# A Mamba stage's start: the first image's statistics loaded ahead of the weights, the second image's placed later

## The chip, the cores and the metric

The kernel runs on one core of a Trainium2 chip. A core has five engines that each work through their own queue of instructions in order: TensorE (PE, with its weight loads PEld), VectorE (DVE), ScalarE (ACT), GpSimd (POOL) and SyncE (SP), which here issues all transfers between DRAM and the core's memory. The engines wait for one another by semaphores. The metric is the device time of one execution in microseconds. Before the change it is 4613.92 us, the median of six runs (4610.43 to 4615.99).

## The reference

The input x holds two images of 256 channels and 64 x 64 positions, so 4096 positions ("tokens") each. Two layers follow one another; cut to what matters:

```python
x = x + mamba(group_norm(x))       # layer 0
x = x + attention(group_norm(x))   # layer 1

def mamba(v):                                  # tokens (B, L, C)
    yn = layer_norm(v) * gamma + beta
    xm, z = split(yn @ W_in.T)                 # 512 channels each
    u = silu(conv1d_4_taps(xm) + conv_b)
    proj = u @ W_xp.T                          # dt (16), B (16), C (16)
    dt = softplus(proj[..., :16] @ W_dt.T + b_dt)
    h = exp(dt * A) * h + dt * u * B           # scan over the 4096 tokens, 16 states a channel
    ym = (sum_n(h * C) + u * D) * silu(z)
    y2 = ym @ W_out.T + yn
    return gelu(y2 @ W1.T + b1) @ W2.T + b2 + y2
```

group_norm takes mean and variance over groups of 8 channels and all 4096 positions of an image. So nothing of an image can be normalised before all of that image has been read once. The second image's statistics are needed only when the second image is reached.

## The kernel before

`mamba_stage` handles layer 0 for both images, `attention_block` layer 1 for each image in turn. In `mamba_stage` an image is cut into 8 tiles of 512 tokens; the 16 tiles follow one another, and the scan's state is carried from tile to tile.

The stage begins with a part written straight down: SP issues the loads of all weights and small vectors (L337 to L354, then the permutation matrix, W_dt and the pick matrix at L362, L376 and L382), and VectorE, ScalarE and GpSimd prepare constants from them: neg_a, the negative exponential of A_log (L358, L359); diag_d (L364); 16 tap matrices, each the identity times one tap of the convolution (L369); w_dt, split into a rounded half and a rest (L379, L380); pick (L383). Three of these sources sit for a while in the three buffers of the ring r_yn, which later hold the tiles' normalised inputs yn.

All further work is handed to a planner (class Plan). Each task is added with an engine, a due time in scan steps, a cost, what it reads and what it writes. The planner lists the tasks in the order in which a model with these costs would start them: of the tasks of one engine that are ready, the one with the earliest due time goes first, a task with another ScalarE function table counting as later by SWITCH, and none more than HORIZON ahead of the oldest task not yet started. Buffers come from rings of a fixed number. That list fixes the order on every engine; on the chip each engine waits only by semaphores. The costs and due times decide only the order.

`first(b, t, due)` loads tile t of image b into a buffer of r_h (five buffers, later used by the scan's states) and takes two `bn_stats` on VectorE, one for each 128 channels (L321). `group_norm(b, k, due)` aggregates an image's statistics (L412), averages over groups by a matmul with gmat, takes the root on ScalarE (L424, L425), and writes scales. Both images were due at the same early times:

```python
    for b in range(IMAGES):
        for t in range(NT):
            first(b, t, -60 + 10 * b)
```

`front(i)` prepares tile i: load of x into yn (L459), group normalisation (L457), mean over channels by a matmul with lnmat, centring (L471), squares (L474), the second matmul, 1/root (L479, L480), scale and shift (L488, L492), four projections with w_in and convolutions with the taps (`conv`), the projection w_xp, its two copies (L516, L517) and VectorE's rest half (L508), then `softplus` for each of four channel groups (L553 to L575), whose results dt and dtu are stored to DRAM and reloaded with each row repeated (L674). `gate` computes silu(z) (L587). `step(g)` is one of 32 scan steps of a tile: two decays on ScalarE (L710), products with B on GpSimd or VectorE (L716), two scans on VectorE (L721), the product with C on GpSimd (L727), and the sum over states on PE (L751, L753). `back(i)` does the output projection with w_out (L599), the two-layer network with w_1 (L621) and w_2 (L635), the statistics for layer 1, and the store. front(i + 1) is added before tile i's steps, so that it runs beside them.

The attention part takes its exponentials on ScalarE, its matmuls on PE, and sums on VectorE and GpSimd; the change doesn't touch it.

Of the kernel before, what the change touches and what calls it, by code (L numbers as in the profile page):

```python
# [11 lines left out]
F32 = mybir.dt.float32  # L12
# [7 lines left out]
P = 128  # L20
# [3 lines left out]
D = 32  # L24
# [77 lines left out]
class Plan:  # L102
# [26 lines left out]
    def add(self, engine, due, cost, emit, reads=(), writes=(), tables=(), lands=0.0):  # L129


        task = Plan.Task()
        task.engine, task.due, task.cost, task.emit = engine, due, cost, emit
        task.tables, task.lands, task.at = tables, lands, len(self.tasks)
        deps = set()
        reads, writes = list(self.keys(reads)), list(self.keys(writes))
        for key in reads:
            deps.add(self.writer.get(key))
        for key in writes:
            deps.add(self.writer.get(key))  # L140
            deps.update(self.readers.get(key, ()))
        for key in reads:
            self.readers.setdefault(key, []).append(task)
        for key in writes:
            self.writer[key], self.readers[key] = task, []
        deps -= {None, task}
        task.deps, task.behind = len(deps), []
        task.ready, task.start = 0.0, None
        for dep in deps:
            dep.behind.append(task)  # L150
        task.bufs = list({id(b): b for b, _ in reads + writes}.values())
        for buf in task.bufs:
            if buf.ring and not buf.left:
                buf.turn = buf.ring.asked
                buf.ring.asked += 1
            buf.left += 1
        self.tasks.append(task)
# [89 lines left out]
def mamba_stage(ctx, tc, xs, stats_out, consts, w, outs):  # L247
# [12 lines left out]
    nc = tc.nc  # L260
    ident, gmat, lnmat, eps_t = consts
    IMAGES = len(xs)
    C, L = xs[0].shape
    KC = C // P
    NT = L // T
    DI = w["conv_w"].shape[0]
    KD = DI // P
    R = w["W_dtT"].shape[0]
    NP = w["W_xpT"].shape[1]
    N = (NP - R) // 2  # L270
    HID = w["W1T"].shape[1]
    KH = HID // P
# [6 lines left out]
    NS = LOW + NP  # L279

    wp = ctx.enter_context(tc.tile_pool(name="l0w", bufs=1))
# [4 lines left out]
    def ring(name, bufs, n=1, pool=None, rows=P, dtype=F32, free=False):  # L286
        return Ring(pool or sb, [rows, T] if n == 1 else [rows, n, T], name, bufs, dtype, free)

    mm = ring("mm", 3, pool=ps, free=True)
    r_yn, r_u, r_z = ring("yn", 3, KC), ring("u", KD + 1), ring("z", KD)  # L290
# [7 lines left out]
    r_h, r_y = ring("h", 5, 2), ring("y", 1, pool=ps)  # L298
# [5 lines left out]
    add = plan.add  # L304

    def image_tile(x, t):
        return x.rearrange("(k p) l -> p k l", p=P)[:, :, bass.ts(t, T)]


    stats_in = [wp.tile([P, KC, NT, nc.vector.BN_STATS_DIM], F32, name=f"stats_in{b}") for b in range(IMAGES)]  # L310
    stats_bufs = [Buf(parts=KC * NT, tile=s) for s in stats_in]

    def first(b, t, due):
        xt = Buf(r_h)
        add("SP", due, 0.8, lambda: nc.sync.dma_start(xt.tile, image_tile(xs[b], t)), [], [xt], lands=3.0)
        for k in range(KC):
            add(
                "DVE",
                due,
                0.7,  # L320
                lambda k=k: nc.vector.bn_stats(stats_in[b][:, k, t, :], xt.tile[:, k, :]),  # L321
                [xt],
                [stats_bufs[b][k * NT + t]],
            )


    def load_rows(name, src, k):
        t = wp.tile([P, k, src.shape[1]], F32, name=name)
        nc.sync.dma_start(t, src.rearrange("(k p) f -> p k f", p=P))
        return t  # L330

    def load_vec(name, src, k):
        t = wp.tile([P, k], F32, name=name)
        nc.sync.dma_start(t, src.rearrange("(k p) -> p k", p=P))
        return t

    gamma = load_vec("gamma", w["gamma"], KC)  # L337
    beta = load_vec("beta", w["beta"], KC)
    w_in = load_rows("w_in", w["W_inT"], KC)
    conv_w = wp.tile([P, KD, TAPS], F32, name="conv_w")  # L340
    nc.sync.dma_start(conv_w, w["conv_w"].rearrange("(k p) o t -> p k (o t)", p=P))
    conv_b = load_vec("conv_b", w["conv_b"], KD)
    w_xp = load_rows("w_xp", w["W_xpT"], KD)
    b_dt = load_vec("b_dt", w["b_dt"], KD)
    d_vec = load_vec("d_vec", w["D"], KD)
    neg_a = wp.tile([P, KD, QUAD, NQ], F32, name="neg_a")
    nc.sync.dma_start(neg_a, w["A_log"].rearrange("p (k j q) -> p k j q", k=KD, j=QUAD))
    sum4 = wp.tile([P, PQ], F32, name="sum4")
    nc.sync.dma_start(sum4, w["sum4"])
    w_out = load_rows("w_out", w["W_outT"], KD)  # L350
    w_1 = load_rows("w_1", w["W1T"], KC)
    b_1 = load_vec("b_1", w["b1"], KH)
    w_2 = load_rows("w_2", w["W2T"], KH)
    b_2 = load_vec("b_2", w["b2"], KC)  # L354


# [1 line left out]
    nc.scalar.activation(neg_a, neg_a, AF.Exp)  # L358
    nc.vector.tensor_scalar_mul(neg_a, neg_a, -1.0)  # L359
    diag_d = wp.tile([P, KD, P], F32, name="diag_d")  # L360
    perm = r_yn.make()[:, 0, 0:P]
    nc.sync.dma_start(perm, w["perm"])  # L362
    for k in range(KD):
        nc.vector.tensor_scalar_mul(diag_d[:, k, :], perm, d_vec[:, k : k + 1])  # L364

# [6 lines left out]
    w_dt = wp.tile([NS, 2, DI], F32R, name="w_dt")  # L372
    nc.gpsimd.memset(w_dt.bitcast(F32), 0.0)
    pick = wp.tile([NS, NQ, P], F32R, name="pick")
    w_dt32 = r_yn.make()[:R, 0, :]
    nc.sync.dma_start(w_dt32, w["W_dtT"])  # L376
    for row in (0, LOW):
        rows = slice(row, row + R)
        nc.vector.tensor_copy(w_dt[rows, 0, :], w_dt32)  # L379
        nc.vector.tensor_sub(w_dt[rows, 1, :], w_dt32, w_dt[rows, 0, :].bitcast(F32))  # L380
    pick32 = r_yn.make()[:NS, 0, :]
    nc.sync.dma_start(pick32, w["pick"])  # L382
    nc.vector.tensor_copy(pick.rearrange("r q p -> r (q p)"), pick32)  # L383

    projs = [wp.tile([NS, T], F32R, name=f"proj{i}") for i in range(2)]
    for t in projs:
        nc.gpsimd.memset(t.bitcast(F32), 0.0)
    r_proj.make = itertools.cycle(projs).__next__

# [9 lines left out]
    def matmul(out, pairs):  # L401
        for i, (lhsT, rhs) in enumerate(pairs):
            nc.tensor.matmul(out, lhsT=lhsT, rhs=rhs, start=(i == 0), stop=(i == len(pairs) - 1))  # L403

    def group_norm(b, k, due):

        s = Buf(r_gn)
        p1, p2 = Buf(mm), Buf(mm)
        out = scales_buf[b * KC + k]

        def aggregate():
            nc.vector.bn_aggr(s.tile[:, 0:2], stats_in[b][:, k, :, :].rearrange("p a s -> p (a s)"))  # L412

        def spread():


            nc.vector.tensor_copy(s.tile[:, 2:3], p1.tile[:, 0:1])
            nc.vector.tensor_sub(s.tile[:, 3:4], s.tile[:, 0:1], s.tile[:, 2:3])
            nc.vector.scalar_tensor_tensor(
                s.tile[:, 4:5], s.tile[:, 3:4], s.tile[:, 3:4], s.tile[:, 1:2], ALU.mult, ALU.add  # L420
            )

        def root():
            nc.scalar.activation(s.tile[:, 5:6], p2.tile[:, 0:1], AF.Ln, bias=eps_t)  # L424
            nc.scalar.activation(scales[:, b, k, 1:2], s.tile[:, 5:6], AF.Exp, scale=-0.5)  # L425

        def shift():
            nc.vector.scalar_tensor_tensor(
                scales[:, b, k, 0:1], s.tile[:, 2:3], -1.0, scales[:, b, k, 1:2], ALU.mult, ALU.mult
            )  # L430

        add("DVE", due, 0.4, aggregate, [stats_bufs[b][k * NT + t] for t in range(NT)], [s])
        add("PE", due, 0.4, lambda: matmul(p1.tile[:, 0:1], [(gmat, s.tile[:, 0:1])]), [s], [p1])
        add("DVE", due, 0.6, spread, [p1], [s])
        add("PE", due, 0.4, lambda: matmul(p2.tile[:, 0:1], [(gmat, s.tile[:, 4:5])]), [s], [p2])
        add("ACT", due, 0.6, root, [p2], [s, out], ("exp",))
        add("DVE", due, 0.2, shift, [s], [out])
# [325 lines left out]
            add("DVE", g + 2.5, 0.7, lambda: nc.vector.tensor_mul(d.z[k].tile, y.tile, d.z[k].tile), [y], [d.z[k]])  # L763

    for b in range(IMAGES):
        for t in range(NT):
            first(b, t, -60 + 10 * b)
    for b in range(IMAGES):
        for k in range(KC):
            group_norm(b, k, -48 + 10 * b)  # L770
    front(0)
    for i, d in enumerate(tiles):
        d.z, d.b, d.c, d.dt_rep, d.dtu_rep = [], [], [], {}, {}
# [482 lines left out]
```

## Time and profile before

| | before |
|---|---|
| median of six runs | 4613.92 us |
| the profiled execution's own time | 4613.43 us |
| its span, first to last instruction | 4611.6 us |
| busy: PE | 4304.5 us (93%) |
| busy: VectorE | 3725.0 us (81%) |
| busy: ScalarE | 3658.3 us (79%) |
| busy: GpSimd | 3882.8 us (84%) |
| moved by DMA | 379.67 MB, 82 GB/s over the span |

The profile is one execution taken by the hardware profiler. Busy time of an engine is an average over two stages with different limits: the Mamba stage (the first 2,000 us or so) and attention. Instruction times are in microseconds from the start of the span; a line number is that of the kernel before. In a list of instructions the arrow in square brackets says how long the engine was idle before the group and what ended that. A landing time of a transfer runs from its issue on SP to its completion. Matmul ends are modelled.

### The profile page before, as it was taken

How to read it: one execution, taken by the hardware profiler on the slowest of the kernel's cores; microseconds unless marked ns; L12 is line 12 of the kernel's file. 1: busy time of each engine (PE TensorE's matmuls, PEld its weight loads, DVE VectorE, ACT ScalarE, POOL GpSimd, SP SyncE). 2: the span in 40 equal slices, each digit the busy share in tenths (PEclk: the TensorE clock that was granted, in tenths of full speed). 3: DMA queues.
4: the chain of work that ended last, by engine and by line, in shares of the span. 5: the costliest groups of instructions: out<-in, count | busy, mean ns of one | idle time of the engine just before them, and what ended most of it. 6: DMA issues, size and time to landing. Idle time of an engine off the chain costs nothing.

```text
span 4611.6 us, 55891 instructions
## 1 busy us (share of the span) xinstructions
PE 4304.5 (93%) x18530; PEld 1569.1 (34%) x18530; DVE 3725.0 (81%) x3980; ACT 3658.3 (79%) x4796; POOL 3882.8 (84%) x2251
## 2 busy tenths in 40 slices
PE   4799999999999999888999999999989999999998
PEld 2233333333333333324333333333343333333332
DVE  3999999999999999963777777777747777777777
ACT  3778888888888888752888888888828888888887
POOL 1999999999999999970888888888808888888887
PEclk9899999999999999989999999999999999999999
DMA  5333333333333333317310140101081101401000
GB/s 171 106 103 109 112 122 121 124 124 124 124 120 114 119 124 119 110 42 244 86 48 17 26 95 23 26 17 26 10 259 40 44 17 28 99 17 26 24 23 8
DMA packets 162330, 379.67 MB, mean 82 GB/s; under 512 B 23409, under 2 KB 41585, under 8 KB 153841
## 3 DMA queue, kind: packets, MB, share of 16 engines
q1 hardware_dynamic: 162032, 376.03, 26.8%
q8 instruction: 147, 2.41, 0.2%
q14 instruction: 151, 1.23, 0.1%
HBM read 282.64 MB, written 93.32 MB: 82 GB/s over the span
## 4 chain that ended last, share of the span: by engine, by line
PE 62%; POOL 13%; DVE 10%; issue 7%; DMA 4%; ACT 4%; SPq 0%; POOLq 0%; DVEq 0%; ACTq 0%
PE s L964 27%; PE po L981 22%; POOL h L727 7%; DVE h L721 6%; PE mm L403 5%; POOL dbu L716 4%; DMA xn<-x_dram 2%; PE y L753 2%; PE mm L599 1%; PE mm L635 1%; PE s L887 1%; DVE bn L716 1%; ACT da L710 1%; PE bn L403 1%; ACT L234 1%
## 5 line engine op out<-in xcount | busy, mean ns | idle before, releaser
L972 ACT ACTIVATE e<-s 128x1024 f32<-128x1024 f32 x2048 | 1987.0, 1022 | 303.1 <-PE s L964 303.1
L1002 DVE TENSOR_TENSOR acc<-acc,e 128x1024 f32<-128x1024 f32 x992 | 1219.5, 1229 | 406.0 <-ACT e L972 402.8
L1013 POOL TENSOR_TENSOR acc_p<-acc_p,e 128x1024 f32<-128x1024 f32 x544 | 1300.3, 2390 | 233.5 <-ACT e L972 221.1
L964 PE MATMUL s<-q,k 128*128 128x512 f32 x4096 | 1316.8, 434 | 3.8 <-ACT e L972 2.1
L727 POOL TENSOR_TENSOR h<-h,c 128x1024 f32<-128x1024 f32 x512 | 1205.6, 2368 | 19.4 <-ACT state L724 14.2
L981 PE MATMUL po<-e,v 128*32 128x512 f32 x8192 | 1091.2, 605 | 0.0
L964 PEld LDWEIGHTS s<-q,k 128*128 128x128 f32 x4096 | 613.6, 188 | 1119.3 <-ACT e L972 1113.8
L710 ACT ACTIVATE da<-dt_rep,neg_a 128x512 f32<-128x512 f32 x1024 | 691.9, 701 | 131.9 <-DVE h L721 109.2
L721 DVE TENSOR_TENSOR_SCAN h<-da,state,dbu 128x512 f32<-128x512 f32 x512 | 650.0, 1274 | 80.1 <-POOL dbu L716 68.2
L721 DVE TENSOR_TENSOR_SCAN h<-da,state,bn 128x512 f32<-128x512 f32 x512 | 647.6, 1265 | 13.7
L1011 POOL TENSOR_TENSOR acc_p<-acc_p,e 128x512 f32<-128x512 f32 x416 | 547.9, 1317 | 33.0 <-POOL acc_p L1013 0.6
L716 POOL TENSOR_TENSOR dbu<-dtu_rep,b 128x512 f32<-128x512 f32 x384 | 487.3, 1280 | 8.6 <-DMA dtu_rep<-dtu_dram 6.4
L234 ACT ACT_TABLE_LOAD x331 | 424.7, 1283 | 6.6 <-PEq L1246 0.7
L753 PE MATMUL y<-h,sum 128*32 128x512 f32 x2048 | 379.8, 635 | 41.9 <-POOL h L727 41.8
L403 PE MATMUL bn<-proj,pick 112*128 112x512 f32 x512 | 305.4, 612 | 119.6 <-DVE h L721 119.2
L716 DVE TENSOR_TENSOR bn<-dtu_rep,bn 128x512 f32<-128x512 f32 x512 | 348.9, 681 | 36.0 <-PE bn L403 19.1
L1010 DVE TENSOR_TENSOR acc<-acc,e 128x512 f32<-128x512 f32 x384 | 268.7, 700 | 58.4 <-ACT e L972 37.4
L1004 POOL TENSOR_TENSOR acc_p<-e 128x1024 f32<-128x1024 f32 x32 | 76.4, 2386 | 272.6 <-ACT e L972 272.6
L981 PEld LDWEIGHTS po<-e,v 128*32 128x32 f32 x8192 | 161.5, 108 | 372.9 <-issue 361.6
L403 PE MATMUL mm<-yn,w_in 128*128 128x512 f32 x512 | 261.4, 635 | 10.0 <-ACT yn L492 4.5
L403 PE MATMUL mm<-xm,taps 128*128 128x512 f32 x512 | 237.1, 607 | 16.2 <-POOL xm L539 14.0
L403 PE MATMUL mm<-yn,w 128*128 128x512 f32 x512 | 239.1, 596 | 11.4 <-ACT z L587 10.1
(125 smaller groups left out, 3436.8 us busy)
## 6 DMA issues: line engine op xcount, KB each, us to landing
dt_rep<-dt_dram SPq DMA_DIRECT2D x128, 512.0 KB, 5.2
dtu_rep<-dtu_dram SPq DMA_DIRECT2D x128, 512.0 KB, 5.6
qk_dram<-halves SPq DMA_DIRECT2D x64, 512.0 KB, 5.8
q<-qk_dram SPq DMA_DIRECT2D x128, 256.0 KB, 4.8
k<-qk_dram SPq DMA_DIRECT2D x64, 512.0 KB, 7.7
b<-bc_dram SPq DMA_DIRECT2D x64, 256.0 KB, 3.1
c<-bc_dram SPq DMA_DIRECT2D x64, 256.0 KB, 4.2
dt_dram<-dt SPq DMA_DIRECT2D x64, 256.0 KB, 2.0
```

The lines of the kernel that those rows point to most:

```text
L403: nc.tensor.matmul(out, lhsT=lhsT, rhs=rhs, start=(i == 0), stop=(i == len(pairs) - 1))
L710: nc.scalar.activation(da[j].tile, dt.tile[:, j, :], AF.Exp, scale=scale)
L716: engine.tensor_mul(out.tile, dtu.tile[:, j, :], rows.tile)
L721: nc.vector.tensor_tensor_scan(h.tile[:, j, :], da[j].tile, dbu.tile, initial, ALU.mult, ALU.add)
L727: nc.gpsimd.tensor_tensor(h.tile, h.tile, rows_c.tile.unsqueeze(1).to_broadcast([P, 2, T]), ALU.mult)
L753: nc.tensor.matmul(y.tile[j * PQ : (j + 1) * PQ, :], lhsT=sum4, rhs=pair[j // 2].h.tile[:, j % 2, :], start=False, stop=(qd == NQ - 1),)
L964: nc.tensor.matmul(ps[:, j, :], lhsT=keys[i // NT, kt][:, h, kj : kj + P], rhs=queries[i][:, h, :], start=True, stop=True)
L972: nc.scalar.activation(e, todo[s].s[half], AF.Exp, scale=SCALE)
L981: nc.tensor.matmul(tiles[i].po[h * D : (h + 1) * D, :], lhsT=v[:, c, g * P + h * D : g * P + (h + 1) * D], rhs=todo[s].e[h // 2][:, h % 2, :],
L1002: nc.vector.tensor_add(acc, acc, ea)
L1011: nc.gpsimd.tensor_add(acc_p[:, 1, :], acc_p[:, 1, :], eb[:, 1, :])
L1013: nc.gpsimd.tensor_add(acc_p, acc_p, eb)
```

## The change

Four things change, all in `mamba_stage`.

1. `first(0, t)` no longer makes tasks for the planner: the eight loads and sixteen statistics of image 0 are written straight down, ahead of all loads of weights.
2. The loads of the weights are put in another order: the small vectors of the convolution come first, then w_in, w_xp and the rest; the permutation matrix, W_dt and the pick matrix are loaded in that row and no longer after it. The three large weights w_out, w_1 and w_2 (2.5 MB) are not loaded there but in one planner task, `load_late`, due at -20.
3. The statistics of image 1 are due at -24 and no longer at -50, beside the convolutions of tile 0, which are due at -33 to -21.
4. The group normalisation of image 1 is due at -12 and no longer at -38; image 0's stays at -48.

```diff
     def first(b, t, due):
         xt = Buf(r_h)
-        add("SP", due, 0.8, lambda: nc.sync.dma_start(xt.tile, image_tile(xs[b], t)), [], [xt], lands=3.0)
+        load = lambda: nc.sync.dma_start(xt.tile, image_tile(xs[b], t))
+        stats = lambda k: nc.vector.bn_stats(stats_in[b][:, k, t, :], xt.tile[:, k, :])
+        if b == 0:
+            xt.tile = r_h.make()
+            load()
+            for k in range(KC):
+                stats(k)
+            return
+        add("SP", due, 0.8, load, [], [xt], lands=3.0)
         for k in range(KC):
-            add("DVE", due, 0.7, lambda k=k: nc.vector.bn_stats(...), [xt], [stats_bufs[b][k * NT + t]])
+            add("DVE", due, 0.7, lambda k=k: stats(k), [xt], [stats_bufs[b][k * NT + t]])
+
+    with tc.manual_schedule():
+        for t in range(NT):
+            first(0, t, 0)
...
     gamma = load_vec("gamma", w["gamma"], KC)
     beta = load_vec("beta", w["beta"], KC)
-    w_in = load_rows("w_in", w["W_inT"], KC)
     conv_w = wp.tile([P, KD, TAPS], F32, name="conv_w")
     nc.sync.dma_start(conv_w, w["conv_w"].rearrange("(k p) o t -> p k (o t)", p=P))
     conv_b = load_vec("conv_b", w["conv_b"], KD)
+    w_in = load_rows("w_in", w["W_inT"], KC)
     w_xp = load_rows("w_xp", w["W_xpT"], KD)
     b_dt = load_vec("b_dt", w["b_dt"], KD)
-    d_vec = load_vec("d_vec", w["D"], KD)
     neg_a = wp.tile([P, KD, QUAD, NQ], F32, name="neg_a")
     nc.sync.dma_start(neg_a, w["A_log"].rearrange("p (k j q) -> p k j q", k=KD, j=QUAD))
+    w_dt32 = r_yn.make()[:R, 0, :]
+    nc.sync.dma_start(w_dt32, w["W_dtT"])
+    pick32 = r_yn.make()[:NS, 0, :]
+    nc.sync.dma_start(pick32, w["pick"])
+    d_vec = load_vec("d_vec", w["D"], KD)
+    perm = r_yn.make()[:, 0, 0:P]
+    nc.sync.dma_start(perm, w["perm"])
     sum4 = wp.tile([P, PQ], F32, name="sum4")
     nc.sync.dma_start(sum4, w["sum4"])
-    w_out = load_rows("w_out", w["W_outT"], KD)
-    w_1 = load_rows("w_1", w["W1T"], KC)
     b_1 = load_vec("b_1", w["b1"], KH)
-    w_2 = load_rows("w_2", w["W2T"], KH)
     b_2 = load_vec("b_2", w["b2"], KC)
...
+    late_buf = Buf()
+
+    def load_late():
+        for tile_, name in ((w_out, "W_outT"), (w_1, "W1T"), (w_2, "W2T")):
+            nc.sync.dma_start(tile_, w[name].rearrange("(k p) f -> p k f", p=P))
...
     for b in range(IMAGES):
-        for t in range(NT):
-            first(b, t, -60 + 10 * b)
+        for t in range(NT if b else 0):
+            first(b, t, -24)
     for b in range(IMAGES):
         for k in range(KC):
-            group_norm(b, k, -48 + 10 * b)
+            group_norm(b, k, -12 if b else -48)
+    add("SP", -20, 2.4, load_late, [], [late_buf], lands=12.0)
     front(0)
```

The old places where perm, w_dt32 and pick32 were loaded are removed; the instructions that use them stay.

More of the change, by code (lines that the diff above doesn't have):

```diff
@@ L314, in first @@
         xt = Buf(r_h)
-        add("SP", due, 0.8, lambda: nc.sync.dma_start(xt.tile, image_tile(xs[b], t)), [], [xt], lands=3.0)
-        for k in range(KC):
[L317 to L324, printed above, removed]
+        load = lambda: nc.sync.dma_start(xt.tile, image_tile(xs[b], t))
[7 more added lines that the diff above has]
+        add("SP", due, 0.8, load, [], [xt], lands=3.0)
+        for k in range(KC):
+            add("DVE", due, 0.7, lambda k=k: stats(k), [xt], [stats_bufs[b][k * NT + t]])
+    with tc.manual_schedule():
+        for t in range(NT):
+            first(0, t, 0)
     def load_rows(name, src, k):
@@ L360, in mamba_stage @@
     diag_d = wp.tile([P, KD, P], F32, name="diag_d")
-    perm = r_yn.make()[:, 0, 0:P]
-    nc.sync.dma_start(perm, w["perm"])
     for k in range(KD):
@@ L374, in mamba_stage @@
     pick = wp.tile([NS, NQ, P], F32R, name="pick")
-    w_dt32 = r_yn.make()[:R, 0, :]
-    nc.sync.dma_start(w_dt32, w["W_dtT"])
     for row in (0, LOW):
@@ L380, in mamba_stage @@
         nc.vector.tensor_sub(w_dt[rows, 1, :], w_dt32, w_dt[rows, 0, :].bitcast(F32))
-    pick32 = r_yn.make()[:NS, 0, :]
-    nc.sync.dma_start(pick32, w["pick"])
     nc.vector.tensor_copy(pick.rearrange("r q p -> r (q p)"), pick32)
@@ L388, in mamba_stage @@
     r_proj.make = itertools.cycle(projs).__next__
+    w_out, w_1, w_2 = (
+        wp.tile([P, k, C if name != "w_1" else HID], F32, name=name)
+        for name, k in (("w_out", KD), ("w_1", KC), ("w_2", KH))
+    )
+    late_buf = Buf()
+    def load_late():
+        for tile_, name in ((w_out, "W_outT"), (w_1, "W1T"), (w_2, "W2T")):
+            nc.sync.dma_start(tile_, w[name].rearrange("(k p) f -> p k f", p=P))
     state = wp.tile([P, IMAGES, KD, QUAD, NQ], F32, name="state")
```

## The prediction

> **What bounds the kernel now.** I read the page first, for which engine carries which part of the span. In its slices, the Mamba stage is the first 17 of 40 (115 us each):
>
> ```profile
> POOL 1999999999999999970888888888808888888887
> DVE  3999999999999999963777777777747777777777
> ```
>
> GpSimd is at its limit from the second slice to the seventeenth. The windows by stage say how closely (columns: stretch, length, then busy time and count for PE, PEld, DVE, ACT, POOL, then clock, DMA share, GB/s):
>
> ```profile
> 20.00:30.00 10.00, 0.00 (x0) 0.00 (x0) 8.91 (x19) 0.00 (x0) 0.00 (x0) 1.00 1.05 384
> 30.00:40.00 10.00, 0.00 (x0) 0.00 (x0) 8.84 (x14) 0.00 (x0) 0.00 (x0) 1.00 1.05 386
> ...
> 500.00:700.00 200.00, 186.42 (x574) 69.43 (x573) 186.33 (x201) 170.18 (x274) 198.19 (x128) 0.99 0.32 102
> ```
>
> In the loop GpSimd is busy 198.19 of 200 us. In the start, DMA is full (384 GB/s), VectorE nearly so, and nothing else runs. As a check on the loop: 266 of the L727 multiplications fall in 500 to 1500 us, so a scan step takes 3.76 us. GpSimd's work per step is 2.37 + 0.75 x 1.28 + 12 x 1.27 / 32 = 3.81 us by the rows of L727, L716 and L572 to L575. So GpSimd sets the pace, a tile of 32 steps takes 120 us, and work that starts earlier by x ends earlier by x, as long as GpSimd is kept fed. The attention part (about 1,990 us to the end) is untouched.
>
> So the place to look is the start. The timeline of the first 62 us (start, length, engine, line):
>
> ```profile
> 19.53 0.88 DVE L364 TENSOR_SCALAR diag_d<-yn,d_vec 128x128 f32<-128x128 f32 x4 [8.28 <-DMA yn<-in_perm]
> ...
> 22.98 6.03 DVE L321 BATCH_NORM_STATS2 stats_in<-h 128x6 f32<-128x512 f32 x10
> ...
> 37.49 8.05 DVE L321 BATCH_NORM_STATS2 stats_in<-h 128x6 f32<-128x512 f32 x12 [0.82 <-DMA h<-in_x]
> ...
> 45.46 0.58 DVE L412 BATCH_NORM_AGGREGATE gn<-stats_in 128x2 f32<-128x48 f32 x2
> ...
> 48.70 1.50 ACT L457 ACTIVATE yn<-yn,scales 128x512 f32<-128x512 f32 x2
> ...
> 53.83 1.28 DVE L471 TENSOR_TENSOR yn<-yn,mm 128x512 f32<-128x512 f32 x2 [3.02 <-PE mm L403]
> ...
> 60.67 1.40 DVE L488 SCALAR_TENSOR_TENSOR yn<-yn,gamma,mm 128x512 f32<-128x512 f32 x2 [5.41 <-ACT mm L480]
> ```
>
> VectorE waits 8.28 us for the small loads behind the weights, then takes the 32 statistics of both images in one row, and only then (45.46) aggregates the first image, whose statistics were complete some 11 us earlier. Tile 0 starts at 48.70. The chain of waits over the first 200 us has no other way round:
>
> ```profile
> 14.58 4.92 DMA yn<-in_perm
> ...
> 24.29 5.66 DMA h<-in_x
> ...
> 62.22 29.76 PE mm L403 x64
> ...
> 104.87 7.88 DMA dtu_rep<-dtu_dram
> ```
>
> After the last of these the first VectorE product of the scan begins (110.83), and GpSimd stays above 98% from 112.8 on.
>
> **What the Trainium skill says.** "DMA: Bandwidth & Descriptors", section "Queues, rings and completion order": each DMA engine consumes descriptors in ring order. The trace agrees: all loads are on SP's one queue, and the 512 KB tile issued at 20.44 behind five others landed after 8.2 us, where the later lone ones of L459 land in 3.9. "TensorE: Matmul & The Clock Gate", opening table: VectorE and ScalarE queues are strictly first in, first out; the aggregate behind the second image's 16 statistics agrees. "ScalarE: Activation LUTs", "What ACT_TABLE_LOAD costs": 1283 ns; the trace has 1283. (It adds a drain of 1380 ns; the table load at 90-92 us is followed by the next activation within 0.1 us, so I don't charge it.)
>
> **The change, part by part**, on the clock of the profiled execution.
>
> *First image ahead of the weights.* Eight loads of 512 KB are issued from 1.2 us. A lone one lands in 3.8 us, so the first is there at 5.0, and at 386 GB/s each takes 524288 B / 386 = 1.36 us: the eighth at 14.5. Two statistics a tile (0.65 us apart) keep up; the last ends at 15.9, the aggregates (0.58) at 16.5, against 46.04.
>
> *What now stands between.* In the built program VectorE does the 16 tap matrices next (0.206 each from 3.30 for 16: to 19.8; their small load conv_w comes right behind the eighth tile, about 16, just in time). Then spread, matmul, root, shift as before (46.49 to 48.79: 2.3 us) to 22.1, the exponential of neg_a (0.26) and its product (0.19), then the four w_dt operations (0.86 + 1.40): 24.8. I name these because tile 0's own input load now sits at the end of SP's queue of loads and reuses the buffer of the w_dt source: SP cannot issue it before 24.8, and behind it on SP stand all of image 2's loads and the late weights. The weights and small vectors ahead of it (w_in 2.7 us, pick 0.6, the rest mostly tiny runs, some 4 us: from 4 to 20 us of before DMA was busy 15.1 us for 4.35 MB, which take 11.3 at 386 GB/s) are through at about 22, so VectorE and not DMA decides. It lands 3.9 later: 28.7, where norm begins: 20.0 us ahead of 48.70. The second norm waits for one statistic of image 2 (its shift stands behind it): 1.5 us, of which the mean matmul hides most; mean ends about 33.7, against 53.83.
>
> *Second image beside tile 0.* VectorE's order is now six statistics, the two L471, seven statistics, the two L488, three statistics. The sixth needs image 2's third tile (28.7 + 3 x 1.36 + 1.35 = 34.1): L471 at 34.1, 19.7 ahead. L488 would follow 6.84 later (60.67 - 53.83) at 41.0, but the thirteenth statistic needs image 2's seventh tile, and the three late weights go ahead of the last three tiles on SP: after 28.7, five tiles (6.8), w_out, w_1, w_2 (1.36 + 2.72 + 2.72), two tiles (2.7) make 45.0, plus 0.68: L488 at 45.7. That is 15.0 ahead of 60.67: the queue gives 4.7 us back.
>
> *From there to the scan.* Tile 1's mean matmul (1.88 us) is no longer ahead of the w_xp projection, but the wait for silu (about 0.9) shows instead: 0.9 gained. VectorE's L562 now stands behind tile 1's L471: 0.2 lost. Dt store and reload keep their 13.4 us (97.44 to 110.83): same transfers, same order. ScalarE has two table loads more before the first decay: from the softplus, 93.67 - 16.2 = 77.5, it does two softplus (6.4), squares (1.2), rstd (1.25), two gates (1.4), shifts (1.4) and four table loads (5.1): first decay 94.2, first product of the scan 110.83 - 15.7 = 95.1, so the two loads are just hidden, by the reload of dtu; without that cover they cost their 2.6. Sum: **15.7 us earlier**.
>
> *The first tiles.* ScalarE has five table loads more in all (6.4 us), and at the scan's start more of tile 1 is still to do: about 7 us of PE and 3 us of ScalarE. Between 110 and 230 us PE is busy 87.6 of 120 and ScalarE 88.9, so both have 25 us or more of cover. The engines' orders differ up to some 381 GpSimd instructions (about three tiles) and are identical after. Before, GpSimd idles 12.1 of the 490 us from 110 to 600, so this could give up to 10 us more; with more work left over and more table switches it could cost several. Bounds +8 and -10; I take a loss of 1.2.
>
> *Nothing:* late weights: first read by L599 some 120 us later; POOL's zero fills; b_1 and b_2.
>
> 15.7 - 1.2 = 14.5 us from the profiled execution (4613.43, span 4611.6): 4598.9. The median of the runs shown is 0.5 higher, 4613.92, so 4599.4 us.
>
> **Rivals.**
>
> *A. The late weights don't hold tile 0* (transfers run faster, or VectorE gets its seven statistics in time): L488 at 41, gain 20: 4594. Against it: DMA already runs at 386 GB/s without a hole.
>
> *B. The first tiles eat part.* GpSimd is starved in the first three tiles because ScalarE or PE does the left-over work first. For: one third of ScalarE's order is new there, and before has a hole of 4.8 us between 450 and 480. Gain 4 to 11: 4603 to 4610; below 4 it counts as no change.
>
> *C. The reason given by the change doesn't bind:* the Mamba stage is GpSimd's, 99% busy, so the start would be hidden. Against: GpSimd has under 4 us of work before 97 us. Time 4614.
>
> *D. Slower.* PE's queue: the seventh bn product (step 6, wanted at 95.1 + 6 x 3.76 = 117.7) stands behind tile 1's first convolution, which waits for an xm copy behind eleven decays on ScalarE. I put the convolution's end at 112, 5 us of room. If each of tile 1's four convolutions blocks the scan so, GpSimd stands still; at 14.5 us of new idle it is even, at 25 us 4624. Needs about 6 us per convolution beyond the room.
>
> **How the numbers follow.** Main case, gain 11.5 to 18: 0.62. A, 18 to 22: 0.10. B: 0.18, half of it above 9.2. C, with what B leaves below 4: 0.05. D: 0.05. 0.2% is 9.2 us, about what a measurement tells from no change. Faster: 0.62 + 0.10 + 0.09 = 0.81; slower 0.05; same 0.09 + 0.05 = 0.14. Range: gains of 7 to 20 hold main, most of A and two thirds of B: 4594 to 4607.
>
> **What would show it.** Aggregate of image 1 near 16.5; tile 0's load issued near 24.8, and what it waits for; L471 near 34; L488 near 45.7, waiting for a statistic that waits for DMA; first VectorE product near 95; GpSimd idle from there over 490 us near 12 to 14. Wrong if tile 0's load is issued much later than 25 (each us costs one), or if GpSimd shows holes over 10 us before 500 us.

## The result, and the profile after

The changed kernel takes 4601.52 us, the median of 19 runs (4598.11 to 4605.50), beside 4614.22 us for the kernel before (39 runs, 4607.70 to 4618.36). The ratio is 0.9973, 95% interval 0.9967 to 0.9979: 12.7 us faster, with an interval of 9.7 to 15.2. The forecast was 4599.4 in a range of 4594 to 4607. The profiled execution of the changed kernel took 4597.81 us, its span is 4596.0, against 4613.43 and 4611.6 before: 15.6 us less for this pair. It was faster than each of the 19 runs, so the 12.7 us of the medians are the better figure for the whole.

In the text the images are the first and the second (image 2); in the code, and in the expectations of experiments 2 and 3, the second is image 1. "SPq" in a list of instructions marks an instruction by which SP issues a transfer.

After the change `first` and what follows stand lower in the file: L321 is now L316, L412 L427, L457 L472, L471 L486, L488 L503, L716 L731, L721 L736, L727 L742. The slices of the page, after:

```profile
POOL 2999999999999999960888888888808888888887
DVE  4999999999999999964777777777747778777777
```

The Mamba stage is as full as before and only begins sooner. The stretches of the start and one of the loop (the columns as in the prediction):

```profile
20.00:26.00 6.00, 1.11 (x4) 1.00 (x4) 4.44 (x16) 1.07 (x5) 0.00 (x0) 1.00 0.24 19
26.00:47.00 21.00, 6.69 (x8) 1.67 (x8) 10.15 (x18) 4.10 (x6) 0.00 (x0) 0.76 1.03 371
...
700.00:900.00 200.00, 183.30 (x558) 69.12 (x558) 185.98 (x202) 169.62 (x277) 198.83 (x131) 0.98 0.36 120
```

From 20 to 26 us DMA moves 19 GB/s: nearly nothing is in flight. From 26 to 47 it is full again, and now VectorE waits: it works 10.15 of 21 us. The timeline after:

```profile
16.20 0.58 DVE L427 BATCH_NORM_AGGREGATE gn<-stats_in 128x2 f32<-128x48 f32 x2
...
24.66 0.37 SPq L474 DMA_DIRECT2D yn<-in_x  x1
...
28.66 0.81 ACT L472 ACTIVATE yn<-yn,scales 128x512 f32<-128x512 f32 x1 [6.45 <-issue]
...
34.34 1.27 DVE L486 TENSOR_TENSOR yn<-yn,mm 128x512 f32<-128x512 f32 x2
...
44.28 2.05 DVE L316 BATCH_NORM_STATS2 stats_in<-h 128x6 f32<-128x512 f32 x3 [6.29 <-DMA h<-in_x]
...
46.24 1.39 DVE L503 SCALAR_TENSOR_TENSOR yn<-yn,gamma,mm 128x512 f32<-128x512 f32 x2
...
96.35 0.69 DVE L731 TENSOR_TENSOR bn<-dtu_rep,bn 128x512 f32<-128x512 f32 x1 [6.43 <-DMA dtu_rep<-dtu_dram]
```

The first image's aggregate moved from 45.46 to 16.20, but tile 0's normalisation only from 48.70 to 28.66, its scaling from 60.67 to 46.24, and the scan's first product from 110.83 to 96.35: of 29.3 us won at the aggregate, 14.5 reach the scan. The waits of SP and then of VectorE in the start (us in total, times, longest) name two places where much of the rest stayed:

```profile
SPq L474 <- DVE w_dt L386: 2.7, 1, 2.7
```

```profile
DVE stats_in L316 <- DMA h<-in_x: 15.3, 6, 6.3
```

SP could not issue tile 0's load until VectorE had finished w_dt. And before L503 VectorE stood for statistics of the second image's sixth tile, 6.3 us, and then its seventh, whose transfers stood in the queue behind the large weights. Where the chain of waits had one row of statistics before, it now has the transfers of the second image's third tile, needed ahead of L486, and of its seventh:

```profile
26.09 7.02 DMA h<-in_x
36.66 8.95 DMA h<-in_x
47.78 22.62 PE mm L418 x52
...
83.66 4.33 DMA dt_dram<-dt
...
89.31 7.01 DMA dtu_rep<-dtu_dram
```

### The profile page after: what moved, and what is told of

It is laid out like the page before. It is cut to its first block, busy times and chain, and to the rows that moved or that the text cites. A ratio compares the mean times of both kernels' runs of the same rounds, so it can differ in the third digit from the quotient of the medians.

```text
span 4596.0 us, 55886 instructions
## 1 busy us (share of the span) xinstructions
PE 4301.3 (94%) x18530; PEld 1563.2 (34%) x18530; DVE 3726.0 (81%) x3980; ACT 3666.2 (80%) x4801; POOL 3881.9 (84%) x2251
## 4 chain that ended last, share of the span: by engine, by line
PE 61%; POOL 15%; DVE 9%; issue 8%; DMA 4%; ACT 3%; SPq 0%; POOLq 0%; DVEq 0%; ACTq 0%
PE s L980 27%; PE po L997 22%; POOL h L742 8%; DVE h L736 6%; POOL dbu L731 5%; PE mm L418 4%; DMA xn<-x_dram 2%; PE y L768 2%; PE mm L614 1%; PE s L903 1%; DVE bn L731 1%; PE mm L650 1%; ACT da L725 1%; POOL lw L587 1%; ACT L234 1%
## 5 line engine op out<-in xcount | busy, mean ns | idle before, releaser
L742 POOL TENSOR_TENSOR h<-h,c 128x1024 f32<-128x1024 f32 x512 | 1205.9, 2368 | 16.6 <-ACT state L739 11.8
L736 DVE TENSOR_TENSOR_SCAN h<-da,state,dbu 128x512 f32<-128x512 f32 x512 | 650.2, 1274 | 83.0 <-POOL dbu L731 75.8
L736 DVE TENSOR_TENSOR_SCAN h<-da,state,bn 128x512 f32<-128x512 f32 x512 | 647.6, 1265 | 14.4 <-ACT mm L494 0.5
L731 POOL TENSOR_TENSOR dbu<-dtu_rep,b 128x512 f32<-128x512 f32 x384 | 487.5, 1281 | 12.7 <-DMA dtu_rep<-dtu_dram 12.7
L731 DVE TENSOR_TENSOR bn<-dtu_rep,bn 128x512 f32<-128x512 f32 x512 | 349.1, 682 | 28.8 <-DMA dtu_rep<-dtu_dram 16.4
L1026 DVE TENSOR_TENSOR acc<-acc,e 128x512 f32<-128x512 f32 x384 | 268.7, 700 | 45.3 <-ACT e L988 16.5
L418 PE MATMUL mm<-xm,taps 128*128 128x512 f32 x512 | 234.5, 601 | 17.6 <-POOL xm L554 15.3
```

What stands on the lines that cost most here:

```text
L731: engine.tensor_mul(out.tile, dtu.tile[:, j, :], rows.tile)
L736: nc.vector.tensor_tensor_scan(h.tile[:, j, :], da[j].tile, dbu.tile, initial, ALU.mult, ALU.add)
L742: nc.gpsimd.tensor_tensor(h.tile, h.tile, rows_c.tile.unsqueeze(1).to_broadcast([P, 2, T]), ALU.mult)
```

## The experiments

My theory ("Theory 1" in the expectations): the gain is the earlier start of the scan, carried one to one to the end by a loop that GpSimd paces; and inside the start, two waits of the change's own making (the reused yn buffer, the large weights ahead of image 2's last tiles) give part of it back. Rivals: the loop absorbs shifts of the start; the parts of the change simply add up; the late large weights are what makes the gain. The times below are medians, with the kernel before run on the same chip: 4613.47 us in the first four experiments, 4614.15 in the last four.

**1. The large weights behind all of image 2's tiles.** The planner now places their task after the last of image 2's statistics.

```diff
-    add("SP", -20, 2.4, load_late, [], [late_buf], lands=12.0)
+    add("SP", -20, 2.4, load_late, [stats_bufs[1]], [late_buf], lands=12.0)
```

> The changed kernel with the three large weights (w_out, w_1, w_2) loaded behind all of image 2's tiles and tile 1's input, not between image 2's fifth and sixth tile. Theory 1 (the transfers' queue holds tile 0: L503 waits for a statistic of a tile that stands behind 2.5 MB of weights): the 6.3 us idle of VectorE ahead of the thirteenth statistic goes, L503 starts at about 40.3 in place of 46.24, and as GpSimd paces the loop the whole end comes 5 to 6 us earlier: about 4596 beside 4601.5. Rival (the start is hidden behind the loop's own pace, or the weights only change places and their readers are late): L503 earlier, end unchanged within 2 us.

Measured: 4594.48 us, ratio 0.9961 (0.9947 to 0.9975). The timeline of VectorE in this kernel:

```profile
35.52 4.24 DVE L316 BATCH_NORM_STATS2 stats_in<-h 128x6 f32<-128x512 f32 x7
40.66 1.41 DVE L503 SCALAR_TENSOR_TENSOR yn<-yn,gamma,mm 128x512 f32<-128x512 f32 x2 [0.90 <-ACT mm L495]
```

The seven statistics run in one row, the idle of 6.29 is gone, and L503 starts 5.6 us earlier, now held by ScalarE's root (L495), as tile 0's own chain wants it. The scan's first product comes at 91.25, 5.1 us earlier than in the changed kernel. So the weights' place was on the path.

**2. Image 2 early again**, so that only the first image ahead and the loads' new order are left.

```diff
-            first(b, t, -24)
+            first(b, t, -50)
...
-            group_norm(b, k, -12 if b else -48)
+            group_norm(b, k, -38 if b else -48)
```

> The changed kernel with image 1 (the second) back at its early due times (-50 and -38), so only the first image ahead and the weights' new order are left. Theory 1: VectorE takes the sixteen statistics of image 1 ahead of the shift that tile 0's normalisation needs; norm of tile 0 starts about 38, L503 about 50 beside 46.24, end 4 us later than the changed kernel: about 4605.5. Rival (image 1's place doesn't matter, all gain is from the first image's early load): equal to the changed kernel, 4601.5.

Measured: 4603.65 us, ratio 0.9974 (0.9963 to 0.9984). Tile 0's normalisation and scaling in this kernel's timeline:

```profile
37.75 1.52 ACT L472 ACTIVATE yn<-yn,scales 128x512 f32<-128x512 f32 x2 [15.32 <-DVE scales L443]
...
47.92 1.41 DVE L503 SCALAR_TENSOR_TENSOR yn<-yn,gamma,mm 128x512 f32<-128x512 f32 x2 [3.58 <-ACT mm L495]
```

The normalisation waits 15.32 us for a shift that stands behind sixteen statistics, as expected at 38; L503 is 2 us sooner than I expected, since the chain from centring to scaling, without statistics in it, took 5.0 and not 6.8 us. First product at 100.67, 4.3 later than in the changed kernel. The medians of the two (9.8 and 12.7 us faster than their kernels before) are nearer than their intervals allow to tell apart; the trace tells them apart.

**3. The other half alone:** the kernel before, weights first, with only image 2's due times moved.

```diff
-            first(b, t, -60 + 10 * b)
+            first(b, t, -24 if b else -60)
...
-            group_norm(b, k, -48 + 10 * b)
+            group_norm(b, k, -12 if b else -48)
```

> The kernel before with only image 1's due times changed to -24 and -12; weights first, as before. Theory 1: the first image's statistics end about 34.2, tile 0's normalisation starts about 38, L488 about 50 beside 60.67; end about 10.5 us earlier than before: about 4603.5. So either part alone gives some 9 to 11 us and both together not their sum. Rival (parts add up): it gives only what the changed kernel has over the kernel with image 1 early, some 4 us: 4610.

Measured: 4602.11 us, ratio 0.9977 (0.9968 to 0.9985): 11.4 us faster than before. In its timeline:

```profile
47.64 1.39 DVE L488 SCALAR_TENSOR_TENSOR yn<-yn,gamma,mm 128x512 f32<-128x512 f32 x2
```

Against 60.67 before; the first product is at 98.26. So two changed due times alone bring 12.6 us of the changed kernel's 14.5 at the first product, and the first image ahead with the loads' new order 10.2 (experiment 2). The parts don't add up: each takes one image's sixteen statistics off the way to tile 0, and when both are done other waits decide.

**4. The first image's statistics taken twice.**

```diff
-            for k in range(KC):
+            for k in [*range(KC), *range(KC)]:
                 stats(k)
```

> The changed kernel with each statistic of image 0 taken twice (same values written again): 16 more of 0.65 us on VectorE in the start, a pure delay. The order of constants on VectorE shifts a little, so tile 0's input is issued near 32.7 and its normalisation starts near 36.7 in place of 28.66: 8 us later. Theory 1 (the loop is paced by GpSimd and a shift of the start goes to the end one to one): end 8 us later than the changed kernel, about 4609.5. Rival (the loop has slack that absorbs a shift): under 3 us later.

Measured: 4597.89 us, ratio 0.9972 (0.9960 to 0.9983): not later at all within the noise. This expectation failed. The timeline of this kernel, VectorE and SP:

```profile
25.79 0.87 DVE L372 TENSOR_SCALAR diag_d<-yn,d_vec 128x128 f32<-128x128 f32 x4
...
26.68 0.37 SPq L474 DMA_DIRECT2D yn<-in_x  x1
...
30.99 0.60 DVE L427 BATCH_NORM_AGGREGATE gn<-stats_in 128x2 f32<-128x48 f32 x2
...
45.62 2.04 DVE L316 BATCH_NORM_STATS2 stats_in<-h 128x6 f32<-128x512 f32 x3 [3.03 <-DMA h<-in_x]
47.57 1.39 DVE L503 SCALAR_TENSOR_TENSOR yn<-yn,gamma,mm 128x512 f32<-128x512 f32 x2
```

The aggregate came 14.8 us later, but L503 only 1.3 and the first product 2.0 later (98.37). Two things took up the delay. SP issued tile 0's load at 26.68, at the end of diag_d (26.66) and well ahead of w_dt, which ended at 30.6: here the load followed the release of the permutation matrix's buffer. I had counted on the w_dt source's. And VectorE still waited 3.03 us for the tile behind the weights. So this run is no test of the one-to-one carry, which it was meant for. It does show that the time of the aggregate alone does not set L503: 14.8 us more there cost 1.3, with tile 0's load no longer held by w_dt.

**5. The W_dt source in a buffer of its own.**

```diff
-    w_dt32 = r_yn.make()[:R, 0, :]
+    w_dt32 = wp.tile([R, DI], F32, name="w_dt32")
```

> The changed kernel with the W_dt source in a buffer of its own, so that tile 0's input load needs no free yn buffer. In the changed kernel SP held that load until 24.66, when VectorE had finished w_dt, with DMA nearly idle from 20 to 26 us. Theory 1: SP issues it at about 21.9, and everything up to the first product of the scan comes 2.8 us earlier, L503 at about 43.5; end 2.8 us earlier than the changed kernel, within its noise: 4598.7. Rival (the small loads still fill DMA until then): L503 unchanged at 46.2.

Measured: 4595.19 us, ratio 0.9959 (0.9945 to 0.9973). In its timeline:

```profile
21.24 0.47 SPq L474 DMA_DIRECT2D yn<-in_x  x1
...
41.13 2.05 DVE L316 BATCH_NORM_STATS2 stats_in<-h 128x6 f32<-128x512 f32 x3 [6.30 <-DMA h<-in_x]
43.10 1.39 DVE L503 SCALAR_TENSOR_TENSOR yn<-yn,gamma,mm 128x512 f32<-128x512 f32 x2
```

The load is issued 3.4 us earlier, right behind the last small load, L503 comes 3.1 and the first product 3.5 earlier (92.84). The wait for the tiles behind the weights is as long as in the changed kernel (6.30): the two waits follow one another.

**6. Both repairs.** Edits 1 and 5 together.

> Both repairs: the W_dt source in its own buffer, and the three large weights behind image 2's tiles. Theory 1 (both waits are on the path, one after the other): L503 at about 37.9, first product of the scan about 88.5, the scan loop again 1,930 to 1,936 us long; end about 22 us earlier than before: 4592. Rival (VectorE's own row of constants and statistics is next on the path): L503 at 39 to 40, end as with the weights' repair alone, 4594.5.

Measured: 4589.51 us, ratio 0.9945 (0.9932 to 0.9959). In its timeline:

```profile
37.21 1.39 DVE L503 SCALAR_TENSOR_TENSOR yn<-yn,gamma,mm 128x512 f32<-128x512 f32 x2
...
86.72 0.69 DVE L731 TENSOR_TENSOR bn<-dtu_rep,bn 128x512 f32<-128x512 f32 x1 [5.76 <-DMA dtu_rep<-dtu_dram]
```

L503 is below both expectations. The first product is 24.1 us earlier than before, 9.6 earlier than in the changed kernel and 4.5 earlier than with the weights' repair alone. So both waits were on the path, one after the other.

**7. The large weights in front again**, in the straight part, ahead of tile 0's load; the rest as in the change.

```diff
+    w_out = load_rows("w_out", w["W_outT"], KD)
+    w_1 = load_rows("w_1", w["W1T"], KC)
+    w_2 = load_rows("w_2", w["W2T"], KH)
     b_1 = load_vec("b_1", w["b1"], KH)
...
-    add("SP", -20, 2.4, load_late, [], [late_buf], lands=12.0)
```

> The changed kernel with w_out, w_1, w_2 loaded in the straight part again, ahead of tile 0's input, everything else as in the change: undoes the late loading of the large weights. Theory 1 (DMA stood idle from 20 to 26 us, so the weights fit there, and what hurt was their place ahead of image 2's last tiles): tile 0's normalisation starts about 1 us later, at 29.7, L503 at about 41.8 in place of 46.24, end 4 us earlier than the changed kernel: 4597. Rival (loading the large weights late is what makes the gain): tile 0 is held by 2.5 MB more, 6.8 us, and the end is 4607.

Measured: 4593.19 us, ratio 0.9958 (0.9944 to 0.9972). In its timeline (numbering of this kernel, where the normalisation is L463 and the scaling L494):

```profile
31.19 0.81 ACT L463 ACTIVATE yn<-yn,scales 128x512 f32<-128x512 f32 x1 [8.72 <-DMA yn<-in_x]
...
42.75 1.41 DVE L494 SCALAR_TENSOR_TENSOR yn<-yn,gamma,mm 128x512 f32<-128x512 f32 x2 [0.93 <-ACT mm L486]
```

The normalisation is 2.5 us later than in the changed kernel (I had said 1): behind the weights SP took 5.2 us to issue the two small loads of b_1 and b_2, and tile 0's load was issued at 26.11. The scaling is 3.5 earlier, the first product 3.2 earlier (93.11). So loading the large weights late made nothing of the gain; where the change put them it cost about 3 us. In front, much of their 6.8 us falls into the stretch in which DMA stands idle.

**8. Both repairs, and the loads of sum4, b_1 and b_2 moved into the late task.**

> As both repairs together, and the small loads of sum4, b_1 and b_2 also moved behind image 2's tiles. Theory 1 (SP's own queue of small loads is what holds tile 0's input next): issue at about 20.4, normalisation at 24.3, L503 at about 36.3, end 1.5 us earlier than both repairs alone: about 4590.5. Rival (VectorE is next): no difference to both repairs alone.

Measured: 4588.65 us, ratio 0.9944 (0.9930 to 0.9957). In its timeline (here the normalisation is L474, the scaling L505):

```profile
22.33 0.80 ACT L474 ACTIVATE yn<-yn,scales 128x512 f32<-128x512 f32 x1
...
26.01 0.69 DVE L316 BATCH_NORM_STATS2 stats_in<-h 128x6 f32<-128x512 f32 x1
...
26.85 0.81 ACT L474 ACTIVATE yn<-yn,scales 128x512 f32<-128x512 f32 x1 [3.72 <-DVE scales L445]
...
36.27 1.41 DVE L505 SCALAR_TENSOR_TENSOR yn<-yn,gamma,mm 128x512 f32<-128x512 f32 x2 [1.00 <-ACT mm L497]
```

Tile 0, issued at 18.46, has landed at 22.2, and its first half is normalised 4.0 us earlier than in experiment 6. But the second half waits 3.72 us for its shift (L445). This stands behind the first statistic of image 2, which begins only when VectorE is through w_dt, diag_d and pick (26.01). So the scaling gains 0.9 and the first product 0.6 us: VectorE's row is next, as the rival had it. The time equals that of experiment 6 within the noise.

**All ten kernels together.** From each profile: the start of the scan's first product on VectorE, the end of the last multiplication by C on GpSimd less that start (the loop), and the span less that end (attention and the rest). In the last column the median less that of the kernel before on the same chip.

| kernel | first product | loop | rest | median, change |
|---|---|---|---|---|
| before | 110.83 | 1935.5 | 2565.3 | |
| changed | 96.35 | 1934.4 | 2565.3 | -12.7 |
| 1 weights behind | 91.25 | 1932.6 | 2571.0 | -19.0 |
| 2 image 2 early | 100.67 | 1930.6 | 2571.9 | -9.8 |
| 3 image 2 late only | 98.26 | 1935.0 | 2568.0 | -11.4 |
| 4 statistics twice | 98.37 | 1932.1 | 2565.3 | -15.6 |
| 5 own buffer | 92.84 | 1933.3 | 2570.1 | -19.0 |
| 6 both repairs | 86.72 | 1932.3 | 2565.5 | -24.6 |
| 7 weights in front | 93.11 | 1932.4 | 2564.6 | -21.0 |
| 8 small loads late | 86.11 | 1932.5 | 2568.7 | -25.5 |

The first product moves over 24.7 us; the loop stays within 4.9 us, with no trend that gives a shift back. So the carry to the end of the loop is one to one, which is what experiment 4 failed to test. The medians follow the first product within 3.3 us in every row; a straight line through the ten points falls by 1.04 us at the end for each us at the first product. The rest varies by 7.3 us though its code is the same in all ten: that is why one pair of profiles can't resolve these steps by its spans, and why experiments 1, 5 and 7, whose ratio intervals overlap with that of the changed kernel, are told from it by their traces. The intervals of experiments 6 and 8 lie wholly below that of the changed kernel: these two are faster than it. The new order of the small loads was not tried alone; what it gives is not shown.

## Why the prediction was right

The steps, as put before the result, beside what the profile of the changed kernel shows:

| step | predicted | measured |
|---|---|---|
| aggregate of the first image | 16.5 (its end) | 16.20 to 16.78 |
| tile 0's load issued, waiting for w_dt | 24.8 | 24.66, waiting for w_dt |
| its normalisation | 28.7 | 28.66 |
| centring | 34.1 | 34.34 |
| scaling, waiting for a statistic behind the weights | 45.7 | 46.24, idle 6.29 for that |
| first product of the scan | 95.1 | 96.35 |
| GpSimd idle in the 490 us from the first product on (11.3 before) | 12 to 14 | 8.7 |
| effect of the first tiles' new order | 1.2 lost | loop 1.1 shorter |
| whole, profiled pair | 14.5 | 15.6 |
| whole, medians | 14.5 | 12.7 (9.7 to 15.2) |

The mechanism held, step by step, and the experiments confirm its two inner waits and the carry to the end. That the sum came so close is in part luck, since the errors of single terms cancel. L503 came 0.6 us later than predicted. From there to the first L587 took 34.8 us, where the prediction's terms give 36.1 (36.8 before, less 0.9, plus 0.2), so 1.3 less. The store and reload of dt behind it took 1.9 more. Together this is the 1.2 us by which the first product was late. Its first decay at 94.2 rests on a softplus 16.2 us earlier, where its own terms give 15.9 (15.0 and 0.9); measured were 16.4.

Besides the stretch from L503 to L587, four terms were off.

"The queue gives 4.7 us back": experiment 1 shows 5.6 at L503.

"The weights and small vectors ahead of it ... are through at about 22": DMA's last full stretch ends near 20, and from 20 to 26 it is nearly idle. The conclusion stood (VectorE and not DMA decides), and the idle stretch is the room that experiments 5 to 8 use. I had not asked what it could be used for.

"Dt store and reload keep their 13.4 us": they took 15.3, from L587 at 81.02 to 96.35. The store of dt landed 4.33 us after its issue. In the kernel before it was:

```profile
100.08 2.86 DMA dt_dram<-dt
```

The difference is its distance from the eight loads of B and C. SP issued the store 0.8 us after it was done with the last of them, before the change 2.1 us after. In nine of the ten profiles the store lands 0.6 to 0.7 us after the last of these loads has landed. In experiment 2, where it is issued 1.2 us after that landing, it takes 2.01 us. This is what a store queued behind these loads shows; no run moved the loads alone. "Same transfers, same order" was right, but they stood closer together.

"I take a loss of 1.2" for the first tiles: the sign was wrong as far as the trace tells. GpSimd idles 8.7 of the 490 us from the first product on, where it had idled 11.3, and the loop was 1.1 us shorter, which is within the 4.9 us that it varies over the ten kernels. Five more table loads on ScalarE, 6.4 us, lengthen nothing that shows; the cover that the prediction named held. Rival B is gone with it. Of the others, A (the weights don't hold tile 0) is excluded by experiment 1, C by the table above, and D (PE's queue starves the scan) by the loop's length.

One line was read wrongly: the last transfer of the prediction's chain (104.87, 7.88 us long) lands at 112.75, after the first product of the scan (110.83). That product waited for the reload issued just ahead of it. The sum doesn't use this.

## What to carry to other kernels

In a kernel paced by one engine in a long loop, ask when that engine gets its first work; a microsecond there is a microsecond at the end, and cheap. When a head of line is cleared, look at once for the next one in the same queue: here the loads sent "out of the way" landed ahead of tiles that the critical tile needed, because VectorE takes the statistics and tile 0's own work in one order. And a borrowed buffer is a wait: 2 KB a partition of its own for one small source brought 3.5 us at the first product.

## What the runs showed of the hardware

The same attention code took 2564.6 to 2571.9 us in ten profiled executions. With runs of one kernel spread over 5 to 12 us, single executions can't tell apart versions 5 us apart; the stretches of the trace ahead of the loop can.

How long SP takes to issue a load depends on what is still queued, not on the load alone. The load of image 2's sixth tile, 512 KB, first in the changed kernel, where it stands behind five tiles and the large weights, then in experiment 1, where the weights come later:

```profile
31.31 5.26 SPq L315 DMA_DIRECT2D h<-in_x  x1
```

```profile
31.24 0.37 SPq L315 DMA_DIRECT2D h<-in_x  x1
```

At L503 this wait of SP cost nothing: the transfers in the queue ran back to back meanwhile, at 371 GB/s from 26 to 47 us, and the sixth, seventh and eighth tile landed 1.36 us apart.

The permutation matrix's load, with the same loads ahead of it, took SP 1.5 to 1.8 us in the changed kernel and in experiments 4 to 6, and 0.6 in experiments 1, 2, 7 and 8. Where it was long, w_in landed 4.8 to 5.4 us after the first image's eighth tile, elsewhere 3.2 to 3.3; which caused which is not shown, nor what measure of the queue decides.

SP's next load, sum4, waited 1.3 us for w_in to land. This bears on experiment 8: without sum4, b_1 and b_2 ahead of it SP issued tile 0's load at 18.46, in place of 21.95 in experiment 6. Of these 3.5 us, 2.0 come from w_in, which landed that much earlier in this execution, and 1.5 from the three small loads.
